# A graph-attention kernel on one core: attention 1 walks fixed tiles of the edge list, the preparation runs in the order written, and attention 2's first counts load early

## The chip, the core and the metric

The kernel runs on one core of a Trainium2 chip. The metric is the device time of one execution in microseconds; the median of three executions before the change is 4275.56 us. Five engines run their own instruction streams in order: PE (matrix products), DVE (vector), ACT (activations and copies), POOL (here almost only a generator of indirect DMAs) and SP (a queue of DMAs). They wait for each other by semaphores.

## The reference, cut to what matters

There are 6250 nodes of 128 numbers and 200,000 edges (src, dst), sorted by dst.

```python
h = relu(layernorm(x))
h = gat_layer(h, W1, ...)      # attention 1: 4 heads of 16
h = elu(h)
h = gat_layer(h, W2, ...)      # attention 2: 1 head
x = x + h
h = relu(layernorm(x))
x = x + convolution(h, src, dst, edge_attr_4, edge_attr_8)

def gat_layer(x, W, attn_l, attn_r, bias, src, dst, num_nodes):
    feat = (x @ W).reshape(num_nodes, H, D)
    el = sum(feat * attn_l); er = sum(feat * attn_r)
    e = leaky_relu(el[src] + er[dst], 0.2)
    ee = exp(e - segment_max(e, dst)[dst])
    alpha = ee / segment_sum(ee, dst)[dst]
    return segment_sum(feat[src] * alpha, dst) + bias
```

## The kernel before

Nodes lie in `NB` = 49 blocks of 128. The kernel has four parts, one after the other.

**Preparation.** It loads `x`, normalises it (`stats`, `coefs`), multiplies by `W1` (`features`, driven five steps deep by `through`), and writes `table1`, one row of 76 numbers for each node, with the factors of the attention ready-made. Beside this it searches the sorted `dst`: `segments`, `window_segments`, `fetch_parts` and `count_parts` find where each window of two nodes begins, `block_segments` and `block_firsts` where each block of 128 nodes begins (`first_i`). The order of instructions on DVE and ACT is partly written (`keep`) and otherwise the scheduler's.

**Attention 1.** It is done in two ways side by side. The first `NG` = 29 blocks are sparse. For each block, `load_window` loads 34 tiles of 128 edges, a fixed capacity `CAP` that begins at the block's first edge, read from a register; `gather` issues one indirect DMA on POOL for each tile, which fetches 128 rows of `table1` into `G`; and `attend` works on groups of 8, 8, 8, 8 and 2 tiles (`GROUPS`): a one-hot of the destination (`ohr`, DVE), the destination's factors by a product with the transposed one-hot (`oht`, loaded by `load_low` as a broadcast and compared in `node_hot`), the messages `msg` and their split into `halves`, and the scatter into a PSUM bank `whole()` on PE. `end` copies the bank out once a block; `finish1` turns four blocks at a time into rows for attention 2. Edges that a block's 34 tiles hold beyond the block drop out, as they match no node there.
The other `DENSE1` = 20 blocks are dense (`dense1`): matrices of edge counts between all nodes, which `count` builds for all 49 blocks from windows of edges, are multiplied with ramps of the attention logits. The large instruction there is `up` (L945, DVE). The loop at the end of the quoted code hands out counting steps and dense steps by the share of sparse tiles done.

**Attention 2** is dense for all blocks: pairs of blocks, each of which loads its counts `ct` and runs ramps (`ramp`, L1228, ACT), `up` and `down` (DVE) and products (L1237, PE). A branch (`once_more`, for inputs that the fast way cannot do) lies between attention 1 and attention 2; all engines pass it.

**Convolution.** 1563 tiles of edges again, with their own gathers; the change does not touch it.

`gath` holds 6 groups of 8 gathered tiles, so POOL can run up to 48 gathers ahead of DVE. After the last dense step, attention 1 loads the windows of the remaining blocks (`load_window`, `shift_window`, for b from 32 to 48), which no block of the sparse way uses.

Of the kernel before, what the change touches and what calls it, by code (L numbers as in the profile page):

```python
# [44 lines left out]
GROUPS = ((0, 8), (8, 8), (16, 8), (24, 8), (32, 2))  # L45
K = 34
CAP = P * K
# [6 lines left out]
AHEAD = 4  # L54
DENSE1, LAG_D, AFTER, AFTER_D = 20, 3, 3, 20
# [10 lines left out]
def gnn_kernel(ctx: ExitStack, tc: tile.TileContext, x, src, dst, attr4, attr8,  # L66
               W1, al1, ar1, b1, W2, al2, ar2, b2,
               Wl0, Wl1, Ws0, Ws1, Wm1, Wm2, Wtp, Wf0, Wf1, src_t, dst_t, attr4_t, attr8_t, runs,
# [12 lines left out]
    assert NCHUNK * GP * GK == E and E >= CAP and E % (GP * SEG) == 0  # L81
# [13 lines left out]
    NT = src_t.shape[1]  # L95
    NCH = -(-NT // CT)
# [7 lines left out]
    ps_sm = ps_one.enter_context(tc.tile_pool(name="ps_sm", bufs=2, space=PSUM))  # L104
    ps_pre = ExitStack()
# [43 lines left out]
    def load_x():  # L149
        nc.vector.memset(xt[:, FULL, :], 0.0)  # L150
        for b in range(0, FULL, 8):
            n = min(8, FULL - b)
            (nc.scalar, nc.sync)[b // 8 % 2].dma_start(
                xt[:, b:b + n, :], x[b * P:(b + n) * P, :].rearrange("(b p) f -> p b f", p=P))
        nc.scalar.dma_start(xt[:REST, FULL, :], x[FULL * P:, :])
# [5 lines left out]
    pool = one.enter_context(tc.tile_pool(name="att1", bufs=1))  # L161
    seek = ExitStack()
# [6 lines left out]
    nc.sync.dma_start(di[:, :ROWT], rows)  # L169
    nc.sync.dma_start(di[:GP - 1, ROWT:], rows[1:, :1])  # L170
# [8 lines left out]
    w1_sb = const.tile([D, HD], F32, name="w1_sb")  # L179
    nc.scalar.dma_start(w1_sb, W1)  # L180
    a1_sb = const.tile([HD, 2 * H1], F32, name="a1_sb")
    nc.scalar.dma_start(a1_sb, a1_w)
    load_x()

    first_i = const.tile([1, NB], I32, name="first_i")
    over = const.tile([1, NB], F32, name="over")
# [16 lines left out]
    def segments(i0, i1):  # L203
        for i in range(i0, i1):
            below = find.tile([GP, NC * P], BF16, name="belowc", bufs=2)
            keep(nc.vector.tensor_scalar(below, wstarts, df[:, i * WSEG:i * WSEG + 1], None, op0=OP.is_gt))
            for c in range(NC):
                keep(nc.tensor.matmul(pcount[:, c:c + 1], below[:, c * P:(c + 1) * P], ones_b, start=i + c == 0,
                                      stop=i == NSEG - 1 and c == NC - 1))
# [36 lines left out]
    def block_segments():  # L246
        below = find.tile([GP, NB + 1, NS], F32, name="below")
# [12 lines left out]
    def block_firsts():  # L260
# [9 lines left out]
        first = find.tile([1, NB], F32, name="first")  # L270
        keep(nc.vector.tensor_scalar(first, ends[:, :NB], float(E - CAP), None, op0=OP.min))
        keep(nc.vector.tensor_copy(first_i, first))
        keep(nc.vector.tensor_sub(over, ends[:, 1:], first))
        keep(nc.vector.tensor_scalar(over, over, float(CAP), None, op0=OP.is_gt))
        keep(nc.vector.tensor_sub(n_edges, ends[:, 1:], ends[:, :NB]))

    def find_falls():
        falls = find.tile([GP, ROWT], F32, name="falls")
# [6 lines left out]
        keep(nc.vector.tensor_tensor(over, over, falls_at_all, op=OP.max))  # L285

    def low_parts():
        low_i = find.tile([GP, ROWT], I32, name="low_i")
        keep(nc.vector.tensor_scalar(low_i, di[:, :ROWT], P - 1, None, op0=OP.bitwise_and))
        low = find.tile([GP, ROWT], BF16, name="low")  # L290
        keep(nc.scalar.copy(low, low_i))
        nc.sync.dma_start(dlow.rearrange("(p t) -> p t", p=GP), low)
# [3 lines left out]
    def window_start(b):  # L296
        return nc.values_load(
            first_i[0:1, b:b + 1], engines=[SP], min_val=0, max_val=E - CAP,
            skip_runtime_bounds_check_because="first is clamped to this range where it is computed")


    srcw = pool.tile([P, NB, K], I32, name="srcw")
    dstw = pool.tile([P, NB, K], F32, name="dstw")
    raw_dst = {}

    def load_window(b):
        r = window_start(b)
        nc.sync.dma_start(srcw[:, b, :], src[ds(r, CAP)].rearrange("(p k) -> p k", p=P))
        raw_dst[b] = work.tile([P, K], I32, name="dsti", bufs=AHEAD)
        nc.sync.dma_start(raw_dst[b], dst[ds(r, CAP)].rearrange("(p k) -> p k", p=P))  # L310

    def shift_window(b):
        keep(nc.vector.tensor_scalar(dstw[:, b, :], raw_dst.pop(b), -float(b * P), None, op0=OP.add))
# [55 lines left out]
    def load_low(b):  # L369
        t = aw.tile([P, CAP], BF16, name="oht")  # L370
        nc.sync.dma_start(t, dlow[ds(window_start(b), CAP)].partition_broadcast(P))
        return t

    def node_hot(t):
# [3 lines left out]
        return t.rearrange("n (p k) -> n k p", k=K)  # L378
# [167 lines left out]
    def rows_of(table, b0, n):  # L546
# [4 lines left out]
    w1t = transposed([w1_sb], HD, nc.vector.tensor_copy)  # L551
    ps = small()
    nc.tensor.matmul(ps[:D, :2 * H1], w1t[:HD, 0, :], a1_sb, start=True, stop=True)
    nc.vector.tensor_copy(ext1[:, :HD], w1_sb)
    nc.vector.tensor_copy(ext1[:, HD:], ps[:D, :2 * H1])
# [17 lines left out]
    slot_k = pool.tile([P, P, 2], BF16, name="slot_k")  # L573
    nc.gpsimd.iota(slot_k, pattern=[[1, P], [0, 2]], base=0, channel_multiplier=0,
                   allow_small_or_imprecise_dtypes=True)
    slot_b = pool.tile([P, P], BF16, name="slot_b")
    nc.gpsimd.iota(slot_b, pattern=[[1, P]], base=0, channel_multiplier=0,
                   allow_small_or_imprecise_dtypes=True)
    pq3 = pool.tile([P, NB, 2 * H1, 3], BF16, name="pq3")
# [16 lines left out]
    def stats(i):  # L596
        b0, n = 8 * i, 8 if i < NB // 8 - 1 else NB - 8 * i
# [3 lines left out]
        c = coefs(b0, n, mv)  # L601
        next(c)
        return c

    co = {}
    w = HD + 2 * H1
# [41 lines left out]
    c0 = stats(0)  # L648
    keep(nc.vector.tensor_copy(df, di))
    deque(c0, 0)  # L650
    c1 = stats(1)
    through(0)
    segments(0, 1)
    through(1)
    deque(c1, 0)
    segments(1, 5)
    c2 = stats(2)
    through(2)
    through(3)
    segments(5, 6)  # L660
    deque(c2, 0)
    segments(6, NSEG)
    window_segments()
    for q in range(2):
        fetch_parts(q)
    c3 = stats(3)
    through(4)
    through(5)
    block_segments()
    deque(c3, 0)  # L670
    c4 = stats(4)
    through(6)
    through(7)
    block_firsts()
    deque(c4, 0)
    c5 = stats(5)
    through(8)
    count_parts(0)
    fetch_parts(2)
    deque(c5, 0)  # L680
    low_parts()
    through(9)
    write_table(0, 24)
    through(10)
    count_parts(1)
    fetch_parts(3)
    through(11)
    through(12)
    count_parts(2)
    fetch_parts(4)  # L690
    through(13)
    write_table(24, 40)
    through(14)
    through(15)
    through(16)
    write_table(40, NB)
    pq = pool.tile([P, NB, 2 * H1], F32, name="pq")
    node_factors(pq, er1, H1)
    split3(pre, pq3, pq, [P, NB, 2 * H1])
    for q in range(3, 5):  # L700
        count_parts(q)
    window_rows()
    sel1 = pool.tile([P, NB, H1], F32, name="sel1")
    nc.vector.tensor_scalar(sel1, t1[:, :, HD:HD + H1], STEEP, None, op0=OP.mult)
    wide1 = widely(pool, t1[:, :, HD:HD + H1])
    find_falls()
    w2_sb, a2_sb = load_weights(("w2_sb", W2), ("a2_sb", a2_w))
    pw = small()
    keep(nc.tensor.transpose(pw[:D, :HD], w2_sb, ident[:HD, :HD]))
    w2t = work.tile([D, HD], F32, name="w2t")  # L710
    keep(nc.vector.tensor_copy(w2t, pw[:D, :HD]))
    ps = small()
    keep(nc.tensor.matmul(ps[:HD, :2], w2t, a2_sb, start=True, stop=True))
    ext2 = const.tile([HD, 2], F32, name="ext2")
    keep(nc.vector.tensor_copy(ext2, ps[:HD, :2]))

    seek.close()
    fin = one.enter_context(tc.tile_pool(name="fin1", bufs=1))
    aw = one.enter_context(tc.tile_pool(name="aw", bufs=2))
# [6 lines left out]
    slots = ps_one.enter_context(tc.tile_pool(name="ps_slots", bufs=1, space=PSUM)).tile([P, 512], F32, name="slots")  # L726
    nc.vector.tensor_copy(slots[:, :P], slot_k.rearrange("p k j -> p (k j)").bitcast(F32))
    nc.vector.tensor_copy(slots[:, P:P + P // 2], slot_b.bitcast(F32))
# [13 lines left out]
    NG = NB - DENSE1  # L742
    dn = one.enter_context(tc.tile_pool(name="dn", bufs=2))
# [31 lines left out]
    cut = one.enter_context(tc.tile_pool(name="cut", bufs=1))  # L775
# [33 lines left out]
    gath = one.enter_context(tc.tile_pool(name="gath", bufs=6))  # L809
    build = one.enter_context(tc.tile_pool(name="build", bufs=2))  # L810
# [72 lines left out]
    nc.vector.tensor_copy(over1, over)  # L883
# [141 lines left out]
    def attending(b, s, n, oht):  # L1025
        G = gath.tile([P, SB, R1], F32, tag="G", name="G")
        gather(G, table1, srcw[:, b, s:s + n], n)

        def acc_of():
            if s == 0:  # L1030
# [3 lines left out]
        def end():  # L1034
            if b % 4 == 0:
                kept1["sums"] = fin.tile([P, 4, HD + H1], F32, name="sums1", bufs=2)
# [9 lines left out]

    for b in range(AHEAD):
        load_window(b)
# [563 lines left out]
```

## Time and profile before

| | us |
|---|---|
| median of three runs (4267.46 to 4278.62) | 4275.56 |
| the profiled execution, its own time | 4266.29 |
| its span | 4264.5 |
| first gather of attention 1 starts | 114.45 |
| last gather of attention 1 starts | 1655.72 |
| first product of attention 2 starts | 1718.74 |
| POOL busy with 986 gathers of attention 1 | 1149.5 |
| DVE busy between 114 and 1657 us | 1244.08 |

The profile is of one execution. Times in it are from the start of the span. A line of the timeline gives start, duration, engine, source line, operation, what it writes and reads, and in brackets the idle time of the engine before it and what ended it.

### The profile page before, as it was taken

To read this page: it belongs to the slowest core of one execution; us is meant where nothing else is said; L and a number is where in the kernel's file an instruction comes from. 1 tells how busy PE (TensorE), PEld (TensorE's weight loads), DVE (VectorE), ACT (ScalarE), POOL (GpSimd) and SP (SyncE) were. 2 spreads that over 40 slices of the span, in tenths; PEclk is the share of its full clock that TensorE was granted. 3 is DMA by queue.
4 is the path that set the end of the run, shared out by engine and by line. 5 is a ranking of instruction groups with operands and counts; after the bars stand their busy time and mean duration, and the time that the engine had idled before them with its cause. 6 is when DMAs were issued, how large, how long until landed. Compare 5 with 4: busy or idle time off the path is not lost. (4 is left out here: it accounts for less than half of the span.)

```text
span 4264.5 us, 62159 instructions
## 1 busy us (share of the span) xinstructions
PE 3058.5 (72%) x19331; PEld 2133.9 (50%) x19332; DVE 3570.7 (84%) x6078; ACT 2829.5 (66%) x6395; POOL 2703.0 (63%) x2616
## 2 busy tenths in 40 slices
PE   3365657667767765799996777777777777777777
PEld 3254444444544543688884444444444444444444
DVE  5887868888888875788886999989999998998988
ACT  3456757777777674799995656555555655555655
POOL 3777777777777774100003777777777777777775
PEclk9997868877777776899997888888888888888888
DMA  3555656656666663644441222222222222222221
GB/s 84 163 173 158 171 146 178 174 163 172 184 168 172 170 164 82 248 162 157 166 147 52 62 64 63 62 63 62 64 62 63 62 63 64 62 63 63 63 61 50
DMA packets 413231, 486.83 MB, mean 114 GB/s; under 512 B 251997, under 2 KB 300187, under 8 KB 409165
## 3 DMA queue, kind: packets, MB, share of 16 engines
q1 hardware_dynamic: 293108, 252.64, 20.5%
q0 software_dynamic: 84000, 146.30, 14.4%
q10 hardware_dynamic: 35768, 83.68, 5.2%
q8 instruction: 160, 2.62, 0.3%
q14 instruction: 195, 1.59, 0.1%
HBM read 378.89 MB, written 103.42 MB: 113 GB/s over the span
## 5 line engine op out<-in xcount | busy, mean ns | idle before, releaser
L346 POOL DMA_INDIRECT G<-table,srcc x1563 | 1474.8, 944 | 1003.3 <-DVE kept L1279 527.2
L346 POOL DMA_INDIRECT G<-table,srcw x986 | 1149.5, 1166 | 362.6 <-issue 269.0
L942 ACT ACTIVATE up<-erb,sel 128x512 bf16<-128x512 f32 x980 | 637.0, 723 | 11.8 <-DMA counts<-ca 5.9
L836 ACT CAST ca<-small 128x392 bf16<-128x392 f32 x784 | 350.0, 490 | 239.8 <-PE small L834 221.8
L1373 PE MATMUL whole<-halves,ohr 128*128 128x512 f32 x1563 | 506.8, 463 | 0.7 <-ACT acc L1403 0.7
L1228 ACT ACTIVATE ramp<-erb,sel 128x256 bf16<-128x256 f32 (+1 forms) x1225 | 491.4, 495 | 21.3 <-DVE up L1232 17.4
L1315 ACT ACTIVATE g<-G,a 128x128 f32<-128x128 f32 x1563 | 481.0, 392 | 1.8 <-DMA G<-table,srcc 0.9
L1308 PEld LDWEIGHTS big<-wtp_sb,hid 64*128 64x128 f32 x3126 | 266.1, 251 | 372.4 <-issue 357.5
L958 PE MATMUL up<-up,rc 128*102 128x512 bf16 x980 | 342.7, 507 | 148.6 <-DVE up L945 148.4
L1308 PE MATMUL big<-wtp_sb,hid 64*128 64x128 f32 x3126 | 309.1, 353 | 151.8 <-DVE halves L1362 151.3
L834 PE MATMUL small<-key,lo 128*128 128x98 bf16 x3136 | 295.4, 233 | 129.8 <-ACT ca L836 97.8
L1373 PEld LDWEIGHTS whole<-halves,ohr 128*128 128x128 f32 x1563 | 317.0, 210 | 132.4 <-issue 58.5
L1299 ACT ACTIVATE hid<-layer 128x512 f32<-128x512 f32 x392 | 230.5, 588 | 191.2 <-PE layer L1296 191.2
L1296 PE MATMUL layer<-hid,wm_sb 128*128 128x512 f32 x392 | 342.7, 972 | 12.5 <-ACT hid L1299 11.8
L1296 PE MATMUL layer<-a8t,wm_sb 16*128 16x512 f32 x392 | 230.7, 669 | 153.0 <-ACT hid L1299 141.9
L945 DVE TENSOR_TENSOR up<-up,ctc 128x3584 bf16<-128x3584 bf16 x140 | 282.8, 2021 | 68.2 <-ACT up L942 56.6
L834 PEld LDWEIGHTS <-lo 128*128 128x128 bf16 x3136 | 227.9, 113 | 211.6 <-issue 157.5
L1353 ACT CAST halves<-mess 128x512 fp32r<-128x512 f32 x195 | 114.3, 586 | 329.7 <-DVE mess L1340 329.7
L1345 DVE TENSOR_TENSOR halves<-mess,halves 128x512 fp32r<-128x512 f32 x391 | 267.8, 685 | 60.5 <-ACT halves L1348 43.6
L823 DVE TENSOR_TENSOR lo<-slots,turned 128x2048 bf16<-128x2048 bf16 x196 | 238.6, 1217 | 63.2 <-PE small L834 62.4
L958 PEld LDWEIGHTS <-rc 128*102 128x102 bf16 x980 | 157.9, 165 | 265.3 <-issue 234.4
L1237 PE MATMUL big<-rhs,up 128*128 128x196 bf16 x2401 | 240.6, 250 | 48.2 <-DVE up L1232 38.4
(293 smaller groups left out, 6248.8 us busy)
## 6 DMA issues: line engine op xcount, KB each, us to landing
counts<-ca ACTq DMA_DIRECT2D x196, 392.0 KB
ct<-counts SPq DMA_DIRECT2D x192, 392.0 KB
ctc<-counts SPq DMA_DIRECT2D x1120, 56.0 KB
oht<-dlow SPq DMA_DIRECT2D x29, 1088.0 KB
rc<-rhs SPq DMA_DIRECT2D x70, 358.8 KB
G<-table,srcc POOLq DMA_INDIRECT x1563
G<-table,srcw POOLq DMA_INDIRECT x986
a8t<-attr_rows SPq DMA_DIRECT2D x391, 16.0 KB
```

The source lines that it names most:

```text
L346: nc.gpsimd.indirect_dma_start(out=G[:, c, :], out_offset=None, in_=table, in_offset=bass.IndirectOffsetOnAxis(ap=idx[:, c:c + 1], axis=0))
L834: nc.tensor.matmul(ps[:, k * NKEY:(k + 1) * NKEY], lo[:, a, :, r], ky[:, a, :, r], start=True, stop=True)
L836: nc.scalar.copy(ca[:, :, i * W:(i + WBANK) * W].rearrange("p h (k d) -> p h k d", d=W), ps[:, :WBANK * NKEY].rearrange("p (k h d) -> p h ...
L942: nc.scalar.activation(up[:, i], erb[:, j], AF.Relu, bias=sel1[:, h0 + i, 2 * q + j:2 * q + j + 1], scale=STEEP)
L945: nc.vector.tensor_tensor(by_part, by_part, ct.rearrange("p k a h d -> p h (k a) d"), op=OP.min)
L958: nc.tensor.matmul(sums["ups"][j][:2 * C1, :], r[:, i, c:c + 2 * C1], up[:, i], start=h0 + i == 0, stop=h0 + i == NB - 1)
L1228: nc.scalar.activation(ramp[:, h, :n * P], erb[:, :n * P], AF.Relu, bias=sel2[:, h0 + h, :], scale=STEEP)
L1296: keep(nc.tensor.matmul(ph, w, x[:, :npr * P], start=True, stop=True))
L1308: keep(nc.tensor.matmul(pw[:, c, :], hid[half, j * P:(j + 1) * P], wtp_sb[half].rearrange("x p u -> x (p u)"), start=True, stop=True))
L1315: keep(nc.scalar.activation(g0[:, c], G[:, c, :], AF.Copy, scale=a0[:, c, :]))
L1345: keep(nc.vector.tensor_tensor(ms[:, cs, 1, 1], m, ms[:, cs, 0, 1], op=OP.subtract))
L1373: keep(nc.tensor.matmul(acc, oh[:, c, :], ms[:, c].rearrange("e s h i u -> e (s h i u)"), start=start, stop=stop))
```

## The change

1. **Fixed tiles.** The sparse way no longer loads a window for each block. It takes tiles 0 to 935 of the edge list as they stand (`NT1` = 16 x 58 + 8; all of `srcw` and `raw1` in two loads). A chunk `c` of 16 tiles (the first has 8) is summed against a ring of 128 nodes: node modulo 128. Chunks advance by 64 nodes, so each covers the half of the ring before and the half after its middle. For odd chunks the ring holds a block in its own order (`pq3`), for even chunks the upper half of one block and the lower half of the next (`pqx`). `end` copies each chunk's sums out (`ring`) and adds the halves of two neighbours into a block. `find_astray` checks that the edges lie where this needs them, and `once_more` takes over where they do not.
2. **Preparation in written order.** `manual_schedule` fixes the order on DVE, ACT, PE and SP. `x` is loaded from a copy laid out by partition (`x_t`, made on the host from the input as the other tiled inputs are), its first four blocks first; `stats` works on 4 blocks rather than 8; the search for block starts moves behind the table; `gath` is placed before the preparation's own memory.
3. **Memory.** Pools of attention 1 are opened with `reuse_waits="tile"`.
4. **Counts early.** When the last counting step is done, the counts and logits of attention 2's first pair are loaded into `evens`, within attention 1.

The diff, cut to its core:

```diff
-GROUPS = ((0, 8), (8, 8), (16, 8), (24, 8), (32, 2))
-K = 34
-CAP = P * K
-DENSE1, LAG_D, AFTER, AFTER_D = 20, 3, 3, 20
+DENSE1, LAG_D, AFTER, AFTER_D = 20, 96, 96, 20
+    HT = HALF * E // (N * P)
+    NT1 = HT * 2 * NG + HT // 2
...
+    load_x([(nc.sync, 0, 4)])
     nc.scalar.dma_start(w1_sb, W1)
+    nc.scalar.dma_start(a1_sb, a1_w)
+    load_x([(nc.scalar, 4, 8), (nc.sync, 8, 16)])
+    nc.scalar.dma_start(di[:, :ROWT], rows)
+    nc.scalar.dma_start(di[:GP - 1, ROWT:], rows[1:, :1])
+    load_x([(nc.sync, 16, 24), (nc.scalar, 24, 32), (nc.sync, 32, 40), (nc.scalar, 40, NB)])
+    nc.sync.dma_start(srcw, src_t[:, :NT1])
+    nc.sync.dma_start(raw1, dst_t[:, :NT1 + 1])
...
-    def load_low(b):
-        t = aw.tile([P, CAP], BF16, name="oht")
-        nc.sync.dma_start(t, dlow[ds(window_start(b), CAP)].partition_broadcast(P))
+    def load_low(c):
+        t0, t1 = max(0, HT * c - HT // 2), HT * c + HT // 2
+        t = aw.tile([P, HT * P], BF16, name="oht", bufs=3)[:, :(t1 - t0) * P]
+        nc.sync.dma_start(t, dlow[t0 * P:t1 * P].partition_broadcast(P))
...
+    with tc.manual_schedule(engines={nc.vector.engine, nc.scalar.engine, nc.tensor.engine, SP}):
+        slots_up()
+        extend()
+        stats(0)
+        stats(1)
+        ready()
+        through(0)
...
+        write_table(44, NB)
+        w2_sb, a2_sb = load_weights(("w2_sb", W2), ("a2_sb", a2_w))
+        wide1 = node_numbers()
+        count_parts(3)
+        count_parts(4)
+        window_rows()
+        block_segments()
+        find_astray()
+        find_falls()
+        extend2()
+        block_firsts()
...
         def end():
-            acc, sums = kept1["acc"], kept1["sums"]
-            nc.scalar.copy(sums[:, b % 4, :], acc[:, :HD + H1])
-            nc.vector.tensor_add(sums[:, b % 4, :], sums[:, b % 4, :], acc[:, HD + H1:])
+            acc = kept1["acc"]
+            ring = fin.tile([P, HD + H1], F32, name="ring", bufs=2)
+            nc.scalar.copy(ring, acc[:, :HD + H1])
+            nc.vector.tensor_add(ring, ring, acc[:, HD + H1:])
+            if c:
+                b = (c - 1) // 2
+                part = slice(0, HALF) if c % 2 else slice(HALF, P)
+                if c % 2 and b % 4 == 0:
+                    kept1["sums"] = fin.tile([P, 4, HD + H1], F32, name="sums1", bufs=2)
+                nc.vector.tensor_add(kept1["sums"][part, b % 4, :], kept1["ring"][part], ring[part])
...
+    for g in range(NT1 // SB):
+        t0 = g * SB
+        c = (t0 + HT // 2) // HT
+        if t0 == max(0, HT * c - HT // 2):
+            if c + 2 <= 2 * NG:
+                lows[c + 2] = load_low(c + 2)
+            oht = node_hot(lows.pop(c))
+        step(attending(t0, SB, c, oht))
+        if done == len(steps) and evens is None:
+            building.close()
+            evens = ahead2.enter_context(tc.tile_pool(name="evens", bufs=1, side="right", reuse_waits="tile"))
+            pair0 = pair_counts([evens], 0, [nc.sync] * 2), pair_logits([evens], 0)
...
-    for b in range(NG + AHEAD - 1, NB):
-        if b >= NG + AHEAD:
-            load_window(b)
-        shift_window(b)
...
-            ct = dense.tile([P, 2, NQ, NB, QN], BF16, name="ct")
+            pools = evens, odds
+            ct, erb = (pair_counts(pools, b0, [nc.sync] * 2), pair_logits(pools, b0)) if b0 else pair0
```

## The prediction

> **What bounds the kernel now.** I read the page's slices first, then a table of stretches, POOL's waits, and the timeline at both ends of attention 1.
>
> ```profile
> DVE  5887868888888875788886999989999998998988
> POOL 3777777777777774100003777777777777777775
> 114.00:1657.00 1543.00, 1000.85 (x6993) 712.98 (x6994) 1244.08 (x2246) 1086.13 (x2135) 1178.46 (x1011) 0.79 0.61 167
> 1684.00:1719.00 35.00, 4.41 (x18) 3.84 (x19) 6.26 (x28) 7.76 (x20) 0.00 (x0) 0.50 0.49 162
> ```
>
> A slice is 107 us. Attention 1 fills the first sixteen, attention 2 the next five; the convolution is untouched and I leave its time alone. The two rows of the table have span, then busy us of PE, weight loads, DVE, ACT and POOL. In attention 1 no engine seems full; between 1684 and 1719 us all are nearly idle. POOL's 1178 of 1543 misleads. The next lines are a row of the page's costliest groups, two of POOL's waits between 250 and 1600 us (total, times, longest), and five lines of the timeline:
>
> ```profile
> L346 POOL DMA_INDIRECT G<-table,srcw x986 | 1149.5, 1166 | 362.6 <-issue 269.0
> POOL G L346 <- issue: 232.4, 762, 0.3
> POOL G L346 <- DVE w L389: 41.4, 15, 10.8
> 114.45 0.94 POOL L346 DMA_INDIRECT G<-table,srcw  x1 [6.42 <-PE small L713]
> 156.75 1.22 DVE L823 TENSOR_TENSOR lo<-slots,turned 128x2048 bf16<-128x2048 bf16 x1
> 157.36 0.95 POOL L346 DMA_INDIRECT G<-table,srcw  x1 [0.30 <-issue]
> 1609.69 2.02 DVE L945 TENSOR_TENSOR up<-up,ctc 128x3584 bf16<-128x3584 bf16 x1
> 1610.02 2.50 POOL L346 DMA_INDIRECT G<-table,srcw  x1 [0.30 <-issue]
> ```
>
> Every gather is followed by 0.30 us in which POOL waits for nothing: one gather costs 0.94 + 0.30 = 1.24 us. Adding up the timeline, POOL's real waits within attention 1 are 56 us, none before 650 us. So POOL is occupied for 96% of the stage and sets its length: 986 x 1.244 = 1227, 219 of stretched gathers, 25 fetches of `run` at 1.46 = 36, waits 56: 1538 of the 1543 measured. DVE (81%) is second and sometimes makes POOL wait for buffers.
>
> The end of attention 1, in the timeline:
>
> ```profile
> 1703.80 2.08 PE L1211 MATMUL small<-ident,er 128*128 128x128 f32 x8 [24.08 <-DVEq L503]
> 1716.34 1.09 DVE L1232 TENSOR_TENSOR up<-ramp,ct 128x1792 bf16<-128x1792 bf16 x1 [10.55 <-DMA ct<-counts]
> 1718.74 2.44 PE L1237 MATMUL big<-rhs,up 128*128 128x196 bf16 x14 [9.72 <-DMA rhs<-rhs2d]
> ```
>
> DVE finishes attention 1 at about 1684 us. SP then still loads windows for blocks that the sparse way never uses, about 1.4 us each, up to 1702.8; the branch passes at 1703.8, and then counts and `rhs2` must land.
>
> **Part 1, tiles.** 936 gathers for 986: 50 x 1.244 = 62 us off POOL. Whether the stretch goes too is a choice. A timeline search puts 173 of the 219 us beside `up` L945 (140 of 2.02 us) and 19 beside L377 (29 one-hots of `oht`); L823, nearly as long, stretches nothing. L945 reads two SBUF inputs, L823 one from PSUM. The Trainium skill (SBUF — State Buffer, "Who interferes with whom") says of `tensor_tensor` that it has no 2-port mode and takes only the read side of the port it shares with GpSimd, while descriptor generation needs the write side. By that rule L945 blocks no gather, 1166 ns is the gather's own price, and 50 of them are worth 73 us. The row differs, and decides: the stretch belongs to the 140 `up`, which stay. I take 62.
>
> On DVE the 29 groups of 2 tiles go: rows of 413, 292, 282, 199, 170 and 152 ns, 1.51 us x 29 = 44. So do `dstw` shifts in the stage, 6. Added: 59 ring adds and 58 half adds for 29, near the 216 ns of L1039: 88 x 0.21 = 19; one more group of 8, 3.4. The one-hots of `oht` cover nearly the same edges: 0. Net -28: 1244 becomes 1216. It lies beside POOL, so I count no gain, but it must hold: the stage shortens by more than 2.3%, so DVE's share rises from 81 to about 83%, and where the dense steps are thickest (86.7% in one slice of 100 us) POOL will wait more for buffers. Nothing in the trace sizes that. Ends: no more than now (56) and three times now (165); I take 75, as dense steps per tile rise by only 5%: +19.
> The ring also doubles the places where the single bank `acc` is emptied before PE may scatter again: 30 more ACT copies of 0.22 us, and a wait in PE's order with all products behind it. The row "PE whole L404 <- DVE sums L1039: 4.6, 5, 2.0" says 0.2 us a time now: 30 x 0.2 = 6, beside POOL, so 0. The upper end is in the rivals.
> SP: 29 `oht` loads of 1088 KB become 59 of at most 512 KB, the same bytes, fetched two chunks ahead; 98 small window loads and their register reads go. No gain: no engine waits long for them (6 us).
>
> **Part 2, preparation.** POOL's start is what counts. Before, the table's last DMA is issued at 102.75 and the first gather starts at 114.45, after the preparation's memory is free (it ends 6.42 us of idling, behind L713). After, `gath` does not share that memory, and `srcw` is loaded early: the gather waits for the table and for POOL's 25 window fetches. I walk DVE's new order with the rows of now. Start at 10 us (`ext` at 9.9; now the first `bnst` is at 15.3, waiting for `xt`). 24 blocks of statistics at 0.395, 10 `belowc` at 1.02, five coefficient pairs at 0.45, one `er` wait of 2.6 on ACT: `wseg` at 37 instead of 48.3, helped by the 6.6 us that DVE now waits for `wtp_sb`. Five more groups at 4.9 (1.6 statistics, 0.45, and 2.65 us for `er`, which waits for ACT's four `hp`, `transp` and `t`): 61. Then two counts of 1.9, the rest of the statistics, `low_i`, and five drain steps of 1 to 2.6 us: last table DMA at about 86. POOL's last five fetches wait for the third `count_parts` at 84 to 86 and end at 92. First gather at 91: -23. Bounds: if `er` does not wait for ACT, 70; if the written order waits where the scheduler slid something in, 105.
> A wait is added: `block_firsts` stands last in DVE's order and needs `part_i`, whose fetch is behind 17 gathers on POOL (91 + 21 + 1.3, landing at 116). DVE then begins attention at about 118, later than the 114.8 of now, with all its groups queued behind. POOL's 48 buffers cover it: they last 48 x 1.25 = 60 us, to about 153. Without that cover it would cost the 27 us between.
> `reuse_waits` moves only waits for memory; none but the 6.42 is on the path, and it is counted.
>
> **Parts 3 and 4, between the attentions.** Let X be DVE's end (1684). The window loads go: the branch passes at about X+4 instead of X+20. `ct` and `erb` of pair 0 are there, and in the new order of SP pair 1's counts too are issued before the branch, so `rhs2` is first behind it: first product at X+11 rather than X+35. Gain 24. It can be less: on SP pair 1's eight loads of 392 KB stand between the last writes of `table2` and `rhs2d`, and 3.1 MB at 250 GB/s, the rate of slice 17, are 12 us. Ends 12 and 28.
> The early loads of pair 0 stand ahead of `ctc` on SP: about 10 us for one dense step, covered by POOL's run-ahead; 0.
> `x` for attention 2 comes in long rows: ACT, which is 99.9% busy there, now loses 5.5 us to issuing it (3.75 of it seen as idle). -5; ends 0 and 6.
>
> **Sum.** -23 - 62 + 19 - 24 - 5 = -95. The profiled execution (4266.29) is 9.3 us under the median; the difference applies to both: 4171 by the profile, 4275.6 - 95 = 4180 as a median.
>
> **The rivals.**
> *DVE takes over (chance 0.22).* If DVE keeps its 300 us of idle time in the stage, it goes from 118 by 1216 + 300 to 1634, plus the same 27 of tail: 1661 against 1684. -23 - 24 - 5: about 4224. For: windows at 85 to 88% now. Against: 77 us of that idle time is DVE waiting for G, which a POOL ahead of it removes.
> *POOL starts at 70 and hardly waits (0.15).* -44 - 62 - 26 - 6 = -138: 4138. For: `er`'s wait may be an order between two readers of one bank that falls away.
> *Slower: the ring's bank (0.04).* At 1604.49 ACT copies the bank, but DVE adds only at 1607.57 behind an `up`, and the next scatter starts at 1610: 5.5 us. If each of 30 extra ends holds up PE, then `pe`, DVE's `w` and POOL's buffers by 5.5 us, that is 165 us against 114 of gains without the +19: +51, 4327. It turns the sign from 3.8 us an end. Against: today's 0.2 us.
> *No gain (0.02):* the same at 3.8 us.
>
> The likeliest case has 0.57. The range takes in the first two rivals with their ends: 4122 to 4232. A measurement here can tell about 0.3%, 13 us, from no change: faster 0.93, same 0.03, slower 0.04.
>
> **What would show it.** Right: first gather near 91, last near 1575, gather rows x936 with a mean near 1175 ns, stretched ones still beside `up`; POOL's wait for DVE below 100 us; first product of attention 2 about 11 us after DVE's end; no `DVEq L503` wait of 20 us. Wrong: POOL waiting over 150 us for `w` or `msg` (DVE took over), PE waiting for `ring` (the bank), or a table later than 100 us.

## The result, and the profile after

| | before | after |
|---|---|---|
| median, both kernels run by turns | 4272.24 us | 4210.60 us |
| ratio, 95% interval | | 0.9859 (0.9847 to 0.9872) |
| profiled execution, own time | 4266.29 | 4209.89 |
| span | 4264.5 | 4208.0 |
| first gather / last gather of attention 1 | 114.45 / 1655.72 | 98.11 / 1609.40 |
| X, DVE's end of attention 1 | 1684.23 | 1648.40 |
| first product of attention 2 | 1718.74 | 1658.59 |

The change saves 62 us in the median and 56.5 us in the span of the two profiled executions; the forecast was 95. The time lies in the range (4122 to 4232), about two thirds of the way to the forecast. The lines that answer to those shown of before follow. First the page's slices (a slice is 105 us here), then the table of stretches: span, then busy us of PE, weight loads, DVE, ACT and POOL.

```profile
DVE  5796878888888886888886998999899989899997
POOL 3777776767777672100005777777777777777775
98.00:1610.00 1512.00, 954.45 (x6869) 662.39 (x6870) 1239.30 (x2179) 1073.06 (x2124) 1117.34 (x962) 0.80 0.61 169
1648.00:1659.00 11.00, 2.49 (x11) 2.20 (x12) 3.33 (x10) 5.97 (x16) 0.00 (x0) 0.50 0.67 214
```

The idle stretch between the attentions is 11 us, not 35. Within attention 1, POOL's busy time fell by 61 us, but the stretch from first to last gather fell by only 30. POOL's digits, nearly all 7 before, have 6s in them now. Here are the row of the page's costliest groups and the waits between 250 and 1600 us (total, times, longest); the last two lines are the kernel before's:

```profile
L350 POOL DMA_INDIRECT G<-table,srcw x936 | 1088.0, 1162 | 387.1 <-issue 260.6
POOL G L350 <- issue: 230.1, 750, 1.6
POOL G L350 <- DVE w L394: 84.4, 22, 21.2
DVE oht L382 <- DMA oht<-dlow: 42.3, 19, 6.1
DVE w L396 <- DMA G<-table,srcw: 19.3, 3, 7.5
DVE oht L377 <- DMA oht<-dlow: 6.3, 6, 1.8
DVE w L391 <- DMA G<-table,srcw: 58.1, 16, 9.5
```

There are 50 gathers fewer, of the same mean length (1162 ns for 1166). POOL's wait for a free gather buffer, which the profile puts down to DVE's `w`, has doubled from 41.4 to 84.4 us, and its longest from 10.8 to 21.2. DVE in turn waits for gathered rows only 19 us in the same window, where it was 58, and waits 42 us for `oht`, where it was 6.

The start and the end of attention 1, in the timeline:

```profile
98.11 1.19 POOL L350 DMA_INDIRECT G<-table,srcw  x1 [0.46 <-DMA oht<-dlow]
125.65 0.18 DVE L273 CAST part<-part_i 50x40 f32<-50x40 int32 x1 [6.25 <-DMA part_i<-in_dst,seg_i]
127.51 1.21 DVE L355 TENSOR_TENSOR ohr<-slots,dstw 128x1024 fp32r<-128x1024 bf16 x1
143.57 0.23 DVE L828 TENSOR_SCALAR hi<-run 128x128 int32<-128x128 int32 x1 [14.79 <-DMA run<-runs,wfirst]
145.66 0.22 DVE L396 TENSOR_TENSOR w<-w,G 128x64 f32<-128x64 f32 x1
1653.07 2.08 PE L1106 MATMUL small<-ident,er 128*128 128x128 f32 x8 [9.19 <-DVEq L508]
1656.03 1.09 DVE L1286 TENSOR_TENSOR up<-ramp,ct 128x1792 bf16<-128x1792 bf16 x1 [0.17 <-ACT ramp L1282]
1658.59 1.63 PE L1291 MATMUL big<-rhs,up 128*128 128x196 bf16 x9 [3.44 <-DMA rhs<-rhs2d]
```

The gathers begin 16.3 us earlier. DVE does not: it waits for `part_i`, starts its first group at 127.5 (114.8 before), and then waits 14.8 us for `run`, a fetch that stands on POOL behind 30 gathers. At the other end PE's wait at the branch, 24 us before, has become 9, and attention 2's first `up` waits for ACT and no longer for counts.

The whole difference of the two spans, put together from the timelines:

| | forecast | measured |
|---|---|---|
| first gather | -23 | -16.3 |
| 50 gathers and the 0.30 us behind each | -62 | -62.2 |
| stretched gathers | 0 | -14.1 |
| POOL's waits within the stage (55.9 to 101.5) | +19 | +45.6 |
| POOL's other fetches | 0 | +0.7 |
| from last gather to X (28.5 to 39.0) | 0 | +10.5 |
| from X to attention 2's first product (34.5 to 10.2) | -24 | -24.3 |
| rest of attention 2, to its last product | -5 | +2.5 |
| convolution and end | 0 | +1.1 |
| sum | -95 | -56.5 |

The four rows from the gathers to POOL's other fetches add up to the stretch from first to last gather: before, 1147.2 us of gathers, 29.0 of other fetches, 309.2 of short gaps and 55.9 of waits make 1541.3; after, 1085.8, 29.7, 294.3 and 101.5 make 1511.3.

### The profile page after: what moved, and what is told of

Same layout as the page of the kernel before. It is cut to its first block, busy times and chain, and to the rows that moved or that the text cites. A ratio compares the mean times of both kernels' runs of the same rounds, so it can differ in the third digit from the quotient of the medians.

```text
span 4208.0 us, 61393 instructions
## 1 busy us (share of the span) xinstructions
PE 3025.0 (72%) x19231; PEld 2091.7 (50%) x19232; DVE 3565.3 (85%) x5996; ACT 2829.6 (67%) x6404; POOL 2636.8 (63%) x2567
## 5 line engine op out<-in xcount | busy, mean ns | idle before, releaser
L350 POOL DMA_INDIRECT G<-table,srcw x936 | 1088.0, 1162 | 387.1 <-issue 260.6
L996 PE MATMUL up<-up,rc 128*102 128x512 bf16 x980 | 341.1, 504 | 155.0 <-DVE up L983 154.7
L872 PE MATMUL small<-key,lo 128*128 128x98 bf16 x3136 | 298.8, 234 | 126.9 <-ACT ca L874 92.8
L872 PEld LDWEIGHTS <-lo 128*128 128x128 bf16 x3136 | 229.0, 112 | 215.4 <-issue 165.3
L996 PEld LDWEIGHTS <-rc 128*102 128x102 bf16 x980 | 156.0, 163 | 273.0 <-issue 241.5
L861 DVE TENSOR_TENSOR lo<-slots,turned 128x2048 bf16<-128x2048 bf16 x196 | 238.8, 1218 | 60.9 <-PE small L872 59.8
```

The source lines that it names most:

```text
L350: nc.gpsimd.indirect_dma_start(out=G[:, c, :], out_offset=None, in_=table, in_offset=bass.IndirectOffsetOnAxis(ap=idx[:, c:c + 1], axis=0))
L872: nc.tensor.matmul(ps[:, k * NKEY:(k + 1) * NKEY], lo[:, a, :, r], ky[:, a, :, r], start=True, stop=True)
L996: nc.tensor.matmul(sums["ups"][j][:2 * C1, :], r[:, i, c:c + 2 * C1], up[:, i], start=h0 + i == 0, stop=h0 + i == NB - 1)
```

## The experiments

X stands for DVE's end of attention 1 throughout. The expectations say VectorE, GpSimd, TensorE and ScalarE where the profile has DVE, POOL, PE and ACT. Times are set against a kernel before that was run in the same set. In the first two sets it took 4272.70 and 4267.45 us. In the third set every kernel took about 23% longer, the kernel before too (5246.72). DVE's and ACT's instructions are as long as ever there, PE's products a few per cent longer (L996 528 ns in e18, 504 in the changed kernel, at a granted clock of 0.77 and 0.84), and the waits between the engines are longer. Its runs are used as ratios, and within that set only.

### e1: the dead window loads alone

```diff
-    for b in range(NG + AHEAD - 1, NB):     # in the kernel before
-        if b >= NG + AHEAD:
-            load_window(b)
-        shift_window(b)
```

> The kernel before, without the window loads and shifts for the blocks that the sparse way never uses (those issued after the last step of attention 1; nothing that is read is left out). If the 24 us gained between the attentions are the dead loads and the early counts of pair 0 together, the branch passes at about X+4 instead of X+20 (X is the end of attention 1 on VectorE), but counts and rhs2 still have to be fetched behind it: first product of attention 2 at X+19 rather than X+35, so -16 us: about 4256. Rival: the early counts brought nothing and the dead loads were all of it: -24, 4248. Rival: the transfers behind the branch are what is waited for and the loads were hidden: 0, 4272.

Measured: 4252.85 us, ratio 0.9956 (0.9941 to 0.9972). X is at 1686.55. PE's timeline behind it:

```profile
1690.15 2.08 PE L1207 MATMUL small<-ident,er 128*128 128x128 f32 x8 [8.12 <-DVEq L503]
...
1704.26 1.96 PE L1233 MATMUL big<-rhs,up 128*128 128x196 bf16 x11 [9.28 <-DVE down L1229]
```

The branch passes at X+3.6 and the first product comes at X+17.7. Of the 24.3 us between the attentions 16.8 are the dead loads; the other 7.5 are left for the counts that are there early. This is the first theory, which had the first product at X+19.

### e2: part 4 undone in the program's order

```diff
-            pair0 = pair_counts([evens], 0, [nc.sync] * 2), pair_logits([evens], 0)
...
-            ct, erb = (pair_counts(...), pair_logits(pools, b0)) if b0 else pair0
+            ct, erb = pair_counts(...), pair_logits(pools, b0)
```

> The changed kernel with part 4 undone: counts and logits of attention 2's first pair are fetched behind the branch, ahead of rhs2. By the same sum the first product moves from X+10 to X+19: +8 us, about 4219. The fetch also leaves attention 1, where SP issued it ahead of the counts of two dense steps: if that was not covered there, some of the 8 comes back, and VectorE's waits for ctc near the end fall. Rival: the fetch behind the branch runs beside rhs2 on other queues and costs nothing: 4211.

Measured: 4212.98 us, ratio 0.9855 (0.9836 to 0.9874), no different from the changed kernel. The expectation missed, and the queue of SP in its timeline shows why:

```profile
1552.90 2.85 SPq L1099 DMA_DIRECT2D ct<-counts  x6
...
1632.15 1.75 SPq L1099 DMA_DIRECT2D ct<-counts  x4
...
1651.96 3.50 SPq L1270 DMA_DIRECT2D rhs<-rhs2d  x6
```

The counts are still issued from 1553 us on, some 90 us ahead of the branch. The edit moved the call, but the pool `evens` is still opened as soon as the last counting step is done and its memory free, and the scheduler seems to have lifted the loads to there. So the place of the call brings nothing; that the pool's place in memory brings the 7.5 us is likely, but no run moved the pool back. This run does not undo part 4, which is sized only by what e1 leaves over.

### e3: block starts off DVE's path

```diff
         extend2()
-        block_firsts()
...
+        if g == 30:
+            block_firsts()
```

(with `seg`, `found`, `part_i`, `part` and `ends` in the pool of attention 1)

> The changed kernel with block_firsts moved off the head of attention 1: its seven small VectorE instructions, which need part_i (fetched on GpSimd behind 17 gathers), come after the 30th group instead of before the first. VectorE then starts its first group some 7 us earlier (it waits 6.25 us for part_i now). Theory POOL: gathers set the stage, GpSimd runs ahead with 48 buffers, so the earlier start of VectorE is worth nothing: 4211 within 3. Theory DVE: VectorE is so late at its start that it never catches up and sets the stage's end: -6 to -9, about 4203, with GpSimd's waits for VectorE some 10 us lower.

Measured: 4213.77 us, ratio 0.9863 (0.9845 to 0.9880): nothing. DVE's timeline at the start:

```profile
119.58 1.21 DVE L355 TENSOR_TENSOR ohr<-slots,dstw 128x1024 fp32r<-128x1024 bf16 x1
...
139.40 0.23 DVE L827 TENSOR_SCALAR hi<-run 128x128 int32<-128x128 int32 x1 [17.82 <-DMA run<-runs,wfirst]
...
140.23 0.22 DVE L396 TENSOR_TENSOR w<-w,G 128x64 f32<-128x64 f32 x1
```

The first group starts 8 us earlier. Then `hi` waits for `run`, and the first use of gathered rows comes 5.4 us earlier. By the first group of block 5 even this is gone (353.6 for 351.0). The added wait for `part_i`, which the prediction covered with POOL's 48 buffers, costs nothing that can be seen here.

### e4: `oht` fetched further ahead

```diff
-        t = aw.tile([P, HT * P], BF16, name="oht", bufs=3)
+        t = aw.tile([P, HT * P], BF16, name="oht", bufs=4)
...
-                lows[c + 2] = load_low(c + 2)
+                lows[c + 3] = load_low(c + 3)
```

> The changed kernel with four oht buffers instead of three, and each chunk's node numbers fetched three chunks ahead instead of two. VectorE now waits 42 us in the stage for oht (6 before), and GpSimd's waits grew from 56 to 110 us. Theory: the 512 KB loads stand on SP behind the counts and rows of dense steps and come late; VectorE's groups then come late and GpSimd waits for buffers. Then VectorE's wait for oht falls under 10 us, GpSimd's waits to 70 to 80, and the time by 30 to 40 us: about 4175. Rival: VectorE is late for its own work (82% busy, with the dense steps in thick stretches) and the oht wait only stands where another wait would: VectorE waits for something else, GpSimd's waits stay over 100 us, and the time within 5 us of 4211.

Measured: 4204.71 us, ratio 0.9831 (0.9811 to 0.9851). Waits between 250 and 1600 us, in the traced execution, which with 4221.09 us is the slowest of the five:

```profile
POOL G L350 <- DVE w L394: 89.2, 21, 18.9
...
DVE oht L382 <- DMA oht<-dlow: 31.7, 16, 4.5
```

DVE's wait for `oht` fell by a quarter only, and POOL's for DVE did not fall. The theory that late `oht` loads cost 30 to 40 us by making POOL wait is not borne out, by the trace or by the median. But the wait was only shortened, not removed, so a smaller share stays possible. The time is 6 us under the changed kernel's, with intervals that touch: whether it is a better kernel stays open.

### e5: eight gather buffers

```diff
-    gath = one.enter_context(tc.tile_pool(name="gath", bufs=6))
+    gath = one.enter_context(tc.tile_pool(name="gath", bufs=8))
```

> The changed kernel with eight gather buffers of 8 tiles instead of six (64 tiles of run-ahead instead of 48, some 20 us more). GpSimd waits 110 us for VectorE to free a buffer, in stops of up to 21 us at a few places. Theory bursts: VectorE is late only where a pass of the dense steps ends, and keeps up on average: GpSimd's waits fall to 20 to 50 us, its last gather comes 60 to 90 us earlier and the end of attention 1 (X) as much: about 4140. Theory rate: VectorE has little slack left over the whole stage, so GpSimd runs ahead and its last gather comes earlier, but VectorE's end X stays within 10 us of 1648 and the tail from last gather to X grows by what the gathers gain: about 4205.

Measured: 4224.43 us, ratio 0.9903 (0.9886 to 0.9920): slower than the changed kernel. The last gather comes 12 us earlier (1597.44), but attention 2's first product 7.5 us later (1666.08). It is the theory of rates, and something on top, which DVE's waits between 125 and 1600 us name:

```profile
DVE hi L828 <- DMA run<-runs,wfirst: 41.4, 4, 19.4
```

This wait was 17.9 us in the changed kernel. The longest, 19.4 us, ends at 517 us, and by the first group of block 10 DVE is 22 us behind the changed kernel. The fetches of `run` share POOL with the gathers, in order: the more gathers may run ahead, the more stand in front of a fetch that DVE needs now.

### e6: half of the edge one-hots

```diff
-        oh = one_hot(dl, n, aw.tile([P, SB, P], F32R, name="ohr", bufs=3))
+        kept["n"] = kept.get("n", -1) + 1
+        if kept["n"] % 2 == 0:
+            kept["oh"] = one_hot(dl, n, aw.tile([P, SB, P], F32R, name="ohr", bufs=3))
+        oh = kept["oh"]
```

> The changed kernel with the edge one-hot ohr computed for every second group of 8 tiles only; the next group reuses it (part of the computation is left out). 58 instructions of 1.21 us go from VectorE, 70 us, none of which stretches a gather. Theory rate (VectorE sets the end): X comes 50 to 80 us earlier, about 4145, and GpSimd's waits nearly vanish. Theory bursts with GpSimd as the bound: the 110 us of waits shrink by about a third and nothing else does: -20 to -40, about 4180. If GpSimd alone set the stage: 0.

Measured: 4184.30 us, ratio 0.9802 (0.9786 to 0.9819): 24 us by the ratios for 70 us of DVE's work. That is the size of the second theory, but POOL's waits fell by only 10.6 us of 101.5, not by a third.

### e7: an eighth of the gathers left out

```diff
+        if t0 // SB % 8 == 7:
+            G = kept1["G"]
+        else:
             G = gath.tile([P, SB, R1], F32, tag="G", name="G")
             gather(G, table1, srcw[:, t0:t0 + n], n)
+            kept1["G"] = G
```

> The changed kernel in which every eighth group of 8 tiles reuses the gathered rows of the group before it (part of the computation is left out): 824 gathers instead of 936, 112 x 1.244 = 139 us less of GpSimd's own work, nothing else changes on VectorE. If GpSimd still sets the stage, X comes some 110 to 139 us earlier: about 4085. If VectorE now sets it, GpSimd only waits longer for buffers (its waits go from 110 to over 200 us) and X moves by under 40 us: about 4180 or more.

Measured: 4176.07 us, ratio 0.9793 (0.9771 to 0.9816): 28 us by the ratios, for 139 us of POOL's. POOL's waits between 250 and 1600 us:

```profile
POOL G L350 <- DVE w L394: 129.3, 25, 18.9
POOL G L350 <- DVE msg L399: 55.7, 7, 33.1
POOL G L350 <- DVE far L833: 18.8, 3, 14.7
```

By the same account as above, gathers and gaps fell by 162 us, the stretch of the fewer ones included, and POOL's waits rose by 117. The second theory has the size right: what is taken from POOL it now mostly waits. Whether it is DVE that makes it wait, e8 tests.

### e8: the minimum of `up` left out

```diff
-                    nc.vector.tensor_tensor(by_part, by_part, ct.rearrange(...), op=OP.min)
```

> The changed kernel without the minimum of up and ctc in attention 1's dense steps (part of the computation is left out): 140 instructions of 2.02 us go from VectorE, 283 us. By the trace the stretched gathers (204 us over 936) stand beside this instruction: if it is what stretches them, the gather's mean falls from 1162 to 950 to 990 ns. By the Trainium skill's rule a tensor_tensor does not hold the port against descriptor generation: then the mean stays at 1150 or more. Of the time: with the stretch and GpSimd's waits gone the stage is 936 x 1.245 + 36 + some 20 = 1220 instead of 1511 us, about 3920, unless ScalarE (1090 us busy) or TensorE hold it higher; with the waits gone alone, about 4100.

Measured: 4183.02 us, ratio 0.9795 (0.9768 to 0.9821). The group of gathers, and DVE's longest wait between 250 and 1600 us:

```profile
L350 POOL DMA_INDIRECT G<-table,srcw x936 | 935.0, 999 | 500.4 <-issue 257.8 <-DVE w L394 181.6 <-DVE msg L399 26.0
DVE lo L861 <- PE small L872: 236.8, 92, 10.2
```

The gather's mean fell from 1162 to 999 ns: 153 of the 203 us of stretch came from this instruction, as the prediction had read the timeline, and not as its rule from the Trainium skill (SBUF — State Buffer, "Who interferes with whom") would have it. The section itself marks that sentence as inferred, and says beside it that a `tensor_tensor` with both inputs in SBUF contends with GpSimd's reads. A gather takes its row numbers from `srcw`; whether it is that read which is held back no run here shows. But the time gained is 27 us by the ratios, neither 290 nor 110. With 283 us of DVE's work gone and 153 us of POOL's, POOL waits 118 us more, and DVE now waits 237 us for a buffer that PE's counting products L872 have yet to read.

### The pace of blocks 10 to 28

One measure puts e5 to e8 together. A block is 32 tiles, 4 groups (before, 34 tiles and 5 groups). DVE's instruction `w<-w,G` is there once a group, so its time at the first group of block 10 and of block 28 gives the pace of the second part of the stage. In the timelines of before, the changed kernel, e7 and e8, in this order:

```profile
663.41 0.23 DVE L391 TENSOR_TENSOR w<-w,G 128x64 f32<-128x64 f32 x1
1621.40 0.22 DVE L391 TENSOR_TENSOR w<-w,G 128x64 f32<-128x64 f32 x1
```

```profile
645.53 0.22 DVE L396 TENSOR_TENSOR w<-w,G 128x64 f32<-128x64 f32 x1
1572.91 0.23 DVE L396 TENSOR_TENSOR w<-w,G 128x64 f32<-128x64 f32 x1
```

```profile
618.62 0.22 DVE L396 TENSOR_TENSOR w<-w,G 128x64 f32<-128x64 f32 x1
1544.79 0.22 DVE L396 TENSOR_TENSOR w<-w,G 128x64 f32<-128x64 f32 x1
```

```profile
619.94 0.23 DVE L396 TENSOR_TENSOR w<-w,G 128x64 f32<-128x64 f32 x1
1551.90 0.23 DVE L396 TENSOR_TENSOR w<-w,G 128x64 f32<-128x64 f32 x1
```

The differences are 958, 927, 926 and 932 us. In e2 to e6 they are 926, 923, 935, 919 and 924. So from block 10 on the changed kernel goes at 51.5 us a block, and goes no faster with an eighth of the gathers left out, with half of the one-hots left out, or with the largest instruction of DVE left out. What e6, e7 and e8 gain they have gained before block 10 (16, 27 and 26 us by that line's times), e7 and e8 most of it between blocks 4 and 10. From block 10 on neither POOL nor DVE alone sets the pace.

### f1, e15, e16, e18: what else could hold it

```diff
+        if b % 4 == 3 and s == 16:                       # f1, in the kernel before
+            G = kept1["G"]
```
```diff
-                        for i in range(HS):              # e15: products of up
+                        for i in range(0, HS, 2):
```
```diff
-                    for i in range(HS):                  # e16: two ramps by one instruction
+                    for i in range(0, HS, 2):
+                        m = min(2, HS - i)
...
```
```diff
+        if t0 == 0:                                      # e18
+            X = gath.tile([P, 13, R1], F32, name="late", bufs=1)
+            gather(X, table1, srcw[:, 0:13], 13)
```

> The kernel before with 56 gathers less: in every fourth block the third group of 8 tiles reuses the gathered rows of the group before it (part of the computation is left out); VectorE's and the other engines' work is as it was. It does alone what the forecast counted 62 us for. If GpSimd, occupied for 96% of the stage, sets its length, X (VectorE's end of attention 1) comes 56 x 1.244 = 70 us earlier, about 4203. If the other engines are so near behind it that GpSimd only waits more for buffers, X moves by a quarter of that, as it did in the changed kernel with 112 gathers less: -15 to -25, about 4250, with GpSimd's waits up from 67 to over 100 us.

> The changed kernel with 4 instead of 7 products per half step of the dense sums ups (part of the computation is left out): 420 matmuls of 0.504 us go from TensorE, 212 us of its 950 in the stage, and nothing from the others. If TensorE's order of products is what holds VectorE and ScalarE (they wait for its small and whole banks), X comes 60 to 120 us earlier, about 4120. If it is only one of four engines near their limit, the gain is a quarter or less, as for GpSimd: -20 to -40, about 4180. If TensorE has slack: 0.

> The changed kernel with the dense steps' ramp up written for two source blocks in one ScalarE instruction (with the first one's bias, so part of the computation is changed): 4 instructions instead of 7 for the same elements. Each saves the fixed part of an instruction, some 0.15 to 0.2 us by the 723 ns of 512 elements and the 495 ns of 256 in attention 2: 420 x 0.19 = 80 us of ScalarE's 1090. ScalarE is busy all the time from 1560 to 1600 us. If it sets the second half of the stage, X comes 40 to 80 us earlier, about 4150; if it is one of four, -10 to -25, about 4195.

> The changed kernel with 13 idle gathers into a spare tile ahead of the first: GpSimd's useful work begins 13 x 1.24 = 16 us later, as late as in the kernel before, with everything else as it is. The forecast counted the first gather's time in full. If that is right, X comes 16 us later, 4227. If VectorE, which begins its groups at 127 us in any case, and the later stops decide, GpSimd only loses run-ahead: 0 to +4, about 4212.

Measured, in the third set, as ratios to the kernel before: f1 0.9906 (0.9864 to 0.9948), e15 0.9791 (0.9713 to 0.9868), e16 0.9804 (0.9719 to 0.9888), e18 0.9927 (0.9893 to 0.9961).

f1 gains 49 us (27 to 71) for 70 us of POOL's work, between its two theories. But it does not test a POOL that is occupied for 96% of the stage: in this set POOL waits 446 to 475 us within the stage in each of the four traces, not 56, so what a gather was worth in the kernel before stays open.

e15 and e16 cannot be set against the changed kernel, which was not in this set, and their intervals take in its ratio. Against e18, which is the changed kernel with 13 gathers more, they lie 71 and 64 us lower by the ratios, with intervals that do not meet. Of this the 13 gathers should explain no more than the 21 us by which e18 starts later, so relief of PE and of ACT may each bring something. How much, and where, is not shown: from the 41st to the 111th group the traces have 1116 us for e18 and 1101 for e16, and that of e15 (1140) is of an execution 56 us above its median. e18's own question, what a later first gather costs in the end, stays open too. One thing can be read from its trace, the first use of gathered rows:

```profile
146.61 0.22 DVE L396 TENSOR_TENSOR w<-w,G 128x64 f32<-128x64 f32 x1
```

Its first useful gather is at 119.32 us, against 98.14 in e15, where this instruction comes at 146.33. DVE's first use of gathered rows does not depend on these 21 us.

## Why the prediction came out as it did

**Right in mechanism and size.** The price of a gather, 0.94 us and 0.30 us behind it: 50 of them took 62.2 us off POOL's work. The stretch belongs to `up` and not to the gather (e8), so the mean stayed at 1162 ns. The end of attention 1: 24.3 us for 24, of which e1 shows 16.8 for the dead loads. The bank of the ring costs nothing: PE's wait for `ring` is 2.3 us in the whole stage. The wait for `part_i` is covered (e3).

**The term that was mis-sized: POOL's waits, 19 us forecast, 45.6 measured, with 10.5 us more behind the last gather.** The prediction went from "POOL is occupied for 96% of the stage" to "and sets its length", and charged 19 us because dense steps per tile rise by 5%. To be occupied is not to be far behind the others. The change took 76 us from POOL (62.2 of gathers with their gaps, 14.1 of stretch), and 46 came back as waits. At a larger dose, e7, it was 117 of 162. The forecast needed the pace of the other engines with POOL out of the way. It estimated only DVE's, by busy time, in the rival "DVE takes over". Two of the signs that it listed show the miss: the last gather came at 1609, not near 1575, and POOL's waits for all of DVE's instructions between 250 and 1600 us were some 110 us, not under 100.

**Where the time is missing.** X came 35.8 us earlier. The lines of the pace and X split this in three. At block 10 DVE is 17.9 us ahead, where the earlier first gather and 20 gathers fewer, at 1.244 us each, would make 41. From block 10 to 28 it gains 30.6 us, where 36 gathers fewer would make 45. Behind block 28 it loses 12.7; 40 tiles are left there where there were 34, which would make 7. So over half of the 43 us that are missing is lost before block 10. About 11 us of that is stretch: the gathers of the first ten blocks are stretched by 64 us, before by 53. The rest is DVE falling further behind POOL, which has no wait there until 643 us, as its run-ahead hides this at first. e3 took 5.4 us off DVE's late start and gained nothing, so the late start alone is not the reason; what is wasn't separated.

**The rival "DVE takes over" had the size nearly right and the cause wrong.** It gave 4224 against 4210.6. But DVE did not take over: from block 10 on the pace is the same in e8, where DVE is busy 596 us and not 779. What holds 51.5 us a block is not settled. These are e8's stretch from block 10 to 28 and two of DVE's waits in it:

```profile
620.00:1552.00 932.00, 707.85 (x4561) 443.07 (x4561) 595.99 (x1189) 721.06 (x1417) 574.20 (x582) 0.76 0.64 176
DVE lo L861 <- PE small L872: 181.8, 68, 10.2
DVE oht L382 <- DMA oht<-dlow: 82.4, 26, 6.6
```

DVE waits for PE, ACT is 77% busy and PE 76%, with their waits for each other and for `rc` on top. That points to the chain of small products, copies and loads that pass between them in order. It is only argued. The loads on SP's queue are a rival that no run tested on its own: in the same stretch DVE waits 82 us for `oht`, and e4 shortened that wait only a little.

**Where the 31 us between blocks 10 and 28 came from.** They are there, 958 to 927, but e7 shows that gathers alone would not give more. In the same stretch PE's busy time fell from 667 to 628 us, ACT's from 728 to 713 and DVE's from 794 to 779: the changed kernel has 36 tiles' worth less work on all of them, not only on POOL. Which of these falls was the one that counted wasn't separated.

**Small steps.** First gather: -16.3 for -23. The last fetches of POOL ended at 98, not 92, as the table and the counts of windows came later than the walk through DVE's rows had them. The walk also missed `run`: it stands behind 30 gathers on POOL, and DVE's queue stands behind it for 14.8 us. Stretch: 14.1 us better than forecast, perhaps as 50 gathers fewer can meet an `up`; the prediction had put it at 0, so this part of the gain is luck. Attention 2: 2.5 us worse instead of 5 better. POOL's addition to `x` and the `up` beside it, in the timelines of the changed kernel and of before:

```profile
1681.59 13.84 POOL L1203 TENSOR_TENSOR xt<-xt,b_sb 128x6272 f32<-128x6272 f32 x1 [71.24 <-DMA ct<-counts]
```

```profile
1682.10 14.29 DVE L1286 TENSOR_TENSOR up<-ramp,ct 128x1792 bf16<-128x1792 bf16 x1
```

```profile
1748.09 14.27 POOL L1141 TENSOR_TENSOR xt<-xt,b_sb 128x6272 f32<-128x6272 f32 x1 [91.43 <-DMA ct<-counts]
1749.59 13.71 DVE L1232 TENSOR_TENSOR up<-ramp,ct 128x1792 bf16<-128x1792 bf16 x1 [0.50 <-ACT ramp L1228]
```

An `up` that takes 1.09 us took 14.29, ACT's ramps waited 12.4 us behind it, and nothing that the shorter issue of `x` saved was seen at the end. A like wait of 11.0 us was there before; the prediction counted only the 3.75 us of ACT's idle time that stood beside the issuing.

## What to carry to other kernels

That an engine is occupied for 96% of a stage does not say that work taken from it is paid in full: here 76 us less, 5% of the stage, shortened the time from first to last gather by 30. Before pricing such a cut, ask at what pace the others would go without that engine, and test this by leaving out far more of the work than the change does and comparing the time per block, not the total. Where a load is issued need not follow where it is called: in e2 the moved call changed nothing, so look in the trace for the issue itself. A small fetch that shares an in-order queue with deep run-ahead can be late by the depth of the run-ahead, so more buffers can make a kernel slower (e5).

## What the runs showed of the hardware

A DVE minimum of two SBUF operands (128 x 3584 bf16, 2.02 us) holds back a gather that POOL is issuing; without its 140 instructions 153 us of gather time vanish (e8). The counting comparisons L861, with one operand in PSUM, are 428 us in all and still there in e8, where only 52 us of stretch are left. The reverse is stronger: beside one POOL addition over 128 x 6272 numbers (13.84 us, before 14.27) a DVE minimum of 1.09 us took 14.29 us, before 13.71. No run moved that addition, so this rests on the two traces.
